# Weights of three pairs by VectorE shifts, and the last three pairs weighed in two halves, in a decayed-neighbour graph layer

## The chip, the cores and the metric

The kernel runs on one core of one Trainium2 chip. The metric is the device time of one execution in microseconds (us). The core's engines run side by side, each through its own instructions in order: TensorE (PE) multiplies matrices and transposes, VectorE (DVE) and ScalarE (ACT) work element by element, GpSimd (POOL) does small work in on-chip memory (SBUF), and SyncE (SP) issues DMA transfers. Matmul results land in PSUM, an accumulation memory of a few banks of 512 fp32 columns.

## The reference

```python
def layernorm(x, eps=1e-5):                    # no scale, no shift
    return (x - mean) / sqrt(var + eps)

h = maximum(layernorm(x), 0)                   # x: 4096 x 64
support = h @ weight                           # weight: 64 x 64
mask = (adj != 0)                              # adj: 4096 x 4096, fp32
rank = cumsum(mask, axis=1)
deg = rank[:, -1:]
k = minimum(deg, 100)
pos = rank - (deg - k)
w = mask * where(pos > 0, 0.5 ** (k - pos), 0)
out = x + (w @ support + bias)
```

Each row of `adj` marks neighbours. The last neighbour of a row (highest column) has weight 1, the one before it 1/2, then 1/4, and so on, up to 100 neighbours. The weight of an entry is thus two to the minus (number of neighbours to its right). `adj` is 67 MB in fp32 and is read once; everything else is small.

## The kernel before, in words

**Tiling.** The 4096 rows form 8 groups (g = 0 to 7) of 512 rows, each of four row tiles of 128. The columns are cut in two halves of 2048, and the right half of a group is taken before the left. A group's half is a unit: 16 units u = 0 to 15. A unit is fetched by four loads of 1 MB, one per row tile, so there are 64 loads (n = 0 to 63; loads 60 to 63 belong to unit 15). All loads go out on SP's queue, into a ring of eight buffers (`a_sb`). A load waits until the conversion of the load eight places earlier has freed its buffer.

**Stages of one load.** `convert` (line 339 on VectorE, or line 337 on ScalarE for the numbers listed in `signed`) turns 128x2048 floats into mask bytes. `transpose` (line 350, TensorE) turns four bytes at a time, `settle` (lines 359 and 361, VectorE) copies the result from PSUM to the unit's mask tile `mt`.

**Stages of one unit.** `totals` (line 367, TensorE) counts neighbours in sub-blocks. `split` (line 377, ScalarE) and `divide` (line 380, VectorE) each copy one byte plane of the counts out of PSUM; both read the same bank. For a left half, `carry` (line 386, GpSimd) brings in the count of the right half. `suffix` (line 394, TensorE) sums the counts to the right, `clamp` (line 398, VectorE) limits them. `place` (lines 405 and 410, TensorE) then makes, for four "pairs" of column blocks at once, the number of neighbours to the right of every entry: a PSUM tile `v` per pair, in which two bytes of each word are wanted. A unit has eight pairs, k = 0 to 7, so two places. `weigh` (line 415, ScalarE) turns one pair, 128 x 1024 bytes, into weights `wk` with one Exp instruction. `aggregate` (line 427, TensorE) multiplies a pair's weights by `hr`, the support matrix held as two float32r parts, in two matmuls that add to the group's PSUM bank `acc`. There are five `v` buffers, twelve `wk` buffers, two PSUM buffers under tag "t" (transposes, totals, suffix and output share them), and one `acc`.

**End of a group.** `drain` (lines 438 and 440) copies `acc` to SBUF and adds the bias, `turn_back` (line 447, TensorE) transposes it, `finish` (lines 454 and 455, VectorE) adds the two parts to x. `store` sends the rows out. The last group is drained in two halves, half 0 by ScalarE and half 1 by VectorE, and its two output transfers go out on ScalarE's and SP's queues (line 457).

**Setup.** Meanwhile x is turned (`turn`, `turned`), centred, squared, its variance spread and rooted, multiplied by the weight (`support`), scaled, and split into the parts of `hr` (`first`, `second`). `warm` runs matmuls on a tile of zeros where the plan leaves TensorE idle.

**Order.** A planner in the kernel's own Python decides the order of all instructions before anything runs. Each step is a `task` with an engine, a rank (its place in the stream plus the tables `shift` and `own`), a planned duration and the tasks it needs. The planner repeatedly takes the engine that can start earliest, and on it the task of lowest rank that is ready within a tolerance (`wait`). What comes out is one fixed instruction order per engine. At run time an engine waits at its next instruction until what that needs is there, and everything behind it waits too.

## Time and profile before

| | |
|---|---|
| median of 4 runs | 193.21 us (193.17 to 193.81) |
| profiled execution | 193.29 us |
| its span in the trace | 191.6 us, so 1.7 us lie outside it |
| TensorE busy | 171.5 us (90%) |
| ScalarE busy | 167.5 us (87%), of it 133.0 us in 128 weighs |
| VectorE busy | 153.6 us (80%), of it 81.5 us in 59 conversions |
| GpSimd busy | 12.9 us (7%) |
| moved by DMA | 69.47 MB, mean 363 GB/s over the span |

A group of instructions is named by line, engine and tile; "mean" is the duration of one. In a run of equal instructions the next one starts a little before the one ahead of it has ended, so the spacing of a run is somewhat below the mean duration. The "idle before" of an instruction names what released it. Times such as 168.58 are microseconds from the start of the span.

### The profile page before, as it was taken

How to read it: one execution, taken by the hardware profiler on the slowest of the kernel's cores; microseconds unless marked ns; L12 is line 12 of the kernel's file. 1: busy time of each engine (PE TensorE's matmuls, PEld its weight loads, DVE VectorE, ACT ScalarE, POOL GpSimd, SP SyncE). 2: the span in 40 equal slices, each digit the busy share in tenths (PEclk: the TensorE clock that was granted, in tenths of full speed). 3: DMA queues.
4: the chain of work that ended last, by engine and by line, in shares of the span. 5: the costliest groups of instructions: out<-in, count | busy, mean ns of one | idle time of the engine just before them, and what ended most of it. 6: DMA issues, size and time to landing. Idle time of an engine off the chain costs nothing.

```text
span 191.6 us, 3737 instructions
## 1 busy us (share of the span) xinstructions
PE 171.5 (90%) x1473; PEld 101.3 (53%) x1475; DVE 153.6 (80%) x213; ACT 167.5 (87%) x178; POOL 12.9 (7%) x54
## 2 busy tenths in 40 slices
PE   7799995979999998799999997999999789998971
PEld 2475982435546564556455545465555444664630
DVE  4851479999999988998899979999997999954012
ACT  2379988889899999999969999898699899889970
POOL 7000240100010002000000010000100000001000
PEclk9999999999999999999999999999999999999995
DMA  6999999999999999999999999999999999700200
GB/s 217 416 421 426 414 424 416 424 414 419 424 412 426 421 414 424 421 417 423 419 417 417 428 416 423 423 412 424 417 417 421 416 426 416 318 14 0 82 0 27
DMA packets 10337, 69.47 MB, mean 363 GB/s; under 512 B 1360, under 2 KB 1616, under 8 KB 2128
## 3 DMA queue, kind: packets, MB, share of 16 engines
q1 hardware_dynamic: 10016, 69.15, 87.3%
q8 instruction: 11, 0.18, 0.4%
q10 hardware_dynamic: 304, 0.10, 0.2%
q14 instruction: 6, 0.05, 0.1%
HBM read 68.19 MB, written 1.05 MB: 361 GB/s over the span
## 4 chain that ended last, share of the span: by engine, by line
PE 42%; DVE 27%; ACT 12%; DMA 9%; issue 5%; POOL 3%; ACTq 0%; POOLq 0%; DVEq 0%
PE acc L427 15%; DVE m L339 12%; DMA a_sb<-in_adj_dram 9%; ACT wk L415 9%; PE pt L350 9%; DVE mt L361 5%; PE v L410 4%; PE v L405 4%; ACT sums L377 2%; DVE sums L380 2%; PE pc L263 2%; PE tot L367 2%; PE pd L279 2%; PE po L447 1%; DVE behind L398 1%
## 5 line engine op out<-in xcount | busy, mean ns | idle before, releaser
L415 ACT ACTIVATE wk<-v,floor 128x1024 fp32r<-128x1024 uint8 x128 | 133.0, 1125 | 6.7 <-PE v L410 6.5
L339 DVE TENSOR_SCALAR m<-a_sb 128x2048 uint8<-128x2048 f32 x59 | 81.5, 1385 | 6.0 <-DMA a_sb<-in_adj_dram 6.0
L427 PE MATMUL acc<-wk,hr 128*128 128x512 f32 x256 | 77.9, 423 | 1.6 <-ACT wk L415 0.5
L427 PEld LDWEIGHTS acc<-wk,hr 128*128 128x128 f32 x256 | 43.8, 189 | 15.2 <-issue 5.0
L350 PE MATMUL pt<-ident,m 128*128 128x128 f32 x256 | 41.5, 282 | 6.7 <-DVE m L339 3.1
L361 DVE COPY mt<-pt 128x512 uint32<-128x512 uint32 x59 | 40.1, 680 | 5.7 <-PE pt L350 5.7
L350 PEld LDWEIGHTS pt<-ident,m 128*128 128x128 f32 x256 | 27.8, 141 | 27.2 <-issue 9.6
L405 PE MATMUL v<-behind,where 32*128 32x512 f16 x128 | 15.6, 383 | 1.5 <-DVE behind L398 1.4
L386 POOL COPY sums<-behind 1x512 f16<-1x512 f16 x8 | 5.6, 705 | 141.6 <-ACT sums L377 141.6
L380 DVE CAST sums<-tot 128x512 f16<-128x512 uint8 x16 | 10.9, 684 | 5.0 <-ACT sums L377 4.2
L410 PE MATMUL v<-mt,tri 32*32 32x512 f16 x512 | 14.3, 394 | 0.0
L337 ACT ACTIVATE m<-a_sb 128x2048 int8<-128x2048 f32 x5 | 12.6, 2528 | 0.5 <-DMA a_sb<-in_adj_dram 0.5
L398 DVE TENSOR_SCALAR behind<-ps,excess 128x512 f16<-128x512 f32 x16 | 11.8, 741 | 1.2 <-PE ps L394 1.2
L377 ACT ACTIVATE sums<-tot 128x512 f16<-128x512 uint8 x16 | 9.6, 598 | 2.9 <-DVE sums L380 2.1
L394 PE MATMUL ps<-sums,later 128*128 128x512 f16 x32 | 9.7, 381 | 1.5 <-POOL sums L386 1.4
L367 PE MATMUL tot<-mt,band 128*32 128x512 f16 x128 | 10.2, 393 | 0.4
L410 PEld LDWEIGHTS <-tri 32*32 32x32 f16 x512 | 4.4, 87 | 10.3 <-issue 10.3
L246 PE MATMUL none<-junk 128*128 128x512 bf16 x24 | 8.4, 497 | 1.3 <-DVE junk L131 1.2
L405 PEld LDWEIGHTS <-where 32*128 32x128 f16 x128 | 3.6, 91 | 9.5 <-issue 9.4
L258 ACT ACTIVATE xt<-px 64x512 f32<-64x512 f32 x8 | 4.2, 586 | 4.6 <-PE px L254 4.5
L438 DVE TENSOR_SCALAR acc_part<-acc,bias_sb 128x256 f32<-128x256 f32 x1 | 0.5, 483 | 9.5 <-PE acc L427 9.5
L447 PE MATMUL po<-ident,acc_sb 128*128 128x128 f32 x30 | 4.9, 285 | 2.6 <-ACT acc_sb L440 2.4
(82 smaller groups left out, 81.9 us busy)
## 6 DMA issues: line engine op xcount, KB each, us to landing
a_sb<-in_adj_dram SPq DMA_DIRECT2D x64, 1024.0 KB, 16.7
xr<-in_x_dram SPq DMA_DIRECT2D x2, 512.0 KB, 6.3
out_dram<-xr SPq DMA_DIRECT2D x1, 512.0 KB, 18.7
out_dram<-xr SPq DMA_DIRECT2D x1, 384.0 KB, 2.3
out_dram<-xr ACTq DMA_DIRECT2D x1, 64.0 KB, 1.6
out_dram<-xr SPq DMA_DIRECT2D x1, 64.0 KB, 1.6
w<-in_L_gnn_weight_dram ACTq DMA_DIRECT2D x2, 16.0 KB, 5.9
bias_sb<-in_L_gnn_bias_dram SPq DMA_DIRECT2D x1, 0.2 KB, 17.5
```

The lines of the kernel that those rows point to most:

```text
L337: nc.scalar.activation(m_v.bitcast(I8), a_v, AF.Sign)
L339: nc.vector.tensor_scalar(m_v, a_v, 0.0, 64.0, op0=ALU.not_equal, op1=ALU.add)
L350: nc.tensor.transpose(pts[n][:, c, :], m32[:, c * P:(c + 1) * P], ident)
L361: nc.vector.tensor_copy(mw, pt)
L367: nc.tensor.matmul(tot[SUB * c:SUB * (c + 1), :], band[:, SUB - 12 - 4 * a:2 * SUB - 12 - 4 * a], masks[u][:, c, :, a], start=(a == 0), st ...
L377: nc.scalar.activation(*bytes_of(u, 0), AF.Copy)
L380: nc.vector.tensor_copy(*bytes_of(u, 1))
L398: nc.vector.tensor_scalar(behind[u], pts.pop((u, "s")), excess[UNITS[u][2]], float(MAX_NEIGH), op0=ALU.subtract, op1=ALU.min)
L405: nc.tensor.matmul(v, where[q, a, :], behind[u][q, :], start=True, stop=False, skip_group_check=True)
L410: nc.tensor.matmul(vs[u, 4 * a + j][SUB * c:SUB * (c + 1), :], tri[q, q], m, start=False, stop=True, skip_group_check=True)
L415: nc.scalar.activation(wts[u, k], vs.pop((u, k)).bitcast(U8).rearrange("p (i f) -> p f i", f=4)[:, :2, :], AF.Exp, scale=-LN2, bias=floor)
L427: nc.tensor.matmul(accs[g], hr[:, block(u, k) + 4 * s, :, :].rearrange("p s d -> p (s d)"), wk[:, s, :], start=(k == s == 0 and c0 + cb * ...
```

## The change

ScalarE no longer weighs three of the last sixteen pairs: pair 4 of unit 14 and pairs 0 and 4 of unit 15 (`QUICK`). For each of them VectorE makes the weights in three instructions. `encode` multiplies the counts by -2^23 and limits them at -100 x 2^23, as 32-bit integers; `cut` adds 100 x 2^23; the bits of that integer, read as a float, are a power of two. `take` copies it into a float32r weight tile. The weights come out too large by a fixed power of two, so `lower`, on GpSimd, makes copies of the `hr` blocks of these pairs that are smaller by it, in a freed load buffer, and `gather` aggregates with those.

Pairs 5, 6 and 7 of unit 15 (`PARTED`) are weighed and aggregated in two halves of the 512 rows: first half 0 of all three, then half 1.

Further edits go with it: ScalarE converts two loads in place of five; the turned x lies in a mask buffer and not in a load buffer; the variance lies in the `acc` bank; `support` waits for `power`; the warming matmuls have 256 columns and end at the first `spread`; the planner has new tables and tolerances, so that the order of many instructions moves. The tables `shift` and `own` are replaced as a whole and are left out of the diff.

```diff
+    QUICK = (U - 2, 4), (U - 1, 0), (U - 1, 4)
+    PARTED = 5, 6, 7
...
-    xt = apool.tile([P, N // H], F32, tag="a_sb", name="xt")
+    xt = mpool.tile([P, CB, W, 2], F16, name="mt").rearrange("p c i e -> p (c i e)").bitcast(F32)
...
-    junk = setup.tile([P, W], BF16, name="junk")
+    junk = setup.tile([P, 2 * P], BF16, name="junk")
...
-            nc.tensor.matmul(none, junk[:, :P], junk, start=True, stop=True)
+            nc.tensor.matmul(none[:, :2 * P], junk[:, :P], junk, start=True, stop=True)
...
-            pxs["var"] = ps_v.tile([P, W], F32, tag="v", name="pd")
+            pxs["var"] = ps_a.tile([P, W], F32, tag="acc", name="pd")
...
-    masks, words, wts, accs, tots, pts, sums8, behind, vs, signed = {}, {}, {}, {}, {}, {}, {}, {}, {}, (2, 3, 5, 6, 12)
+    low, codes, masks, words, wts, accs, tots, pts, sums8, behind, vs, signed = {}, {}, {}, {}, {}, {}, {}, {}, {}, {}, {}, (2, 8)
...
-    def weigh(u, k):
+    def weigh(u, k, part=None):
+        r = slice(0, W) if part is None else slice(part * W // 2, (part + 1) * W // 2)
+        if not part:
+            wts[u, k] = wpool.tile([P, 2, W], F32R, name="wk")
+        v = vs[u, k] if part == 0 else vs.pop((u, k))
+        nc.scalar.activation(wts[u, k][:, :, r], v.bitcast(U8).rearrange("p (i f) -> p f i", f=4)[:, :2, r], AF.Exp, scale=-LN2, bias=floor)
+
+    def encode(u, k):
+        both = apool.tile([P, N // H], F32, tag="a_sb", name="code")
+        codes[u, k] = both.rearrange("p (n f i) -> p n f i", n=2, f=2)
+        nc.vector.tensor_scalar(codes[u, k][:, 0].bitcast(I32), vs.pop((u, k)).bitcast(U8).rearrange("p (i f) -> p f i", f=4)[:, :2, :],
+                                -2.0 ** 23, -100 * 2.0 ** 23, op0=ALU.mult, op1=ALU.max)
+
+    def cut(u, k):
+        nc.vector.tensor_scalar(codes[u, k][:, 1].bitcast(I32), codes[u, k][:, 0].bitcast(I32), 100 * 2.0 ** 23, None, op0=ALU.add)
+
+    def take(u, k):
         wts[u, k] = wpool.tile([P, 2, W], F32R, name="wk")
-        nc.scalar.activation(wts[u, k], vs.pop((u, k)).bitcast(U8).rearrange("p (i f) -> p f i", f=4)[:, :2, :], AF.Exp, scale=-LN2, bias=floor)
+        nc.vector.tensor_copy(wts[u, k], codes.pop((u, k))[:, 1])
+
+    def lower(u, k):
+        if not low:
+            both = apool.tile([P, N // H], F32R, tag="a_sb", name="low").rearrange("p (n s e d) -> p n s e d", s=2, e=2, d=D)
+            low.update((uk, both[:, i]) for i, uk in enumerate(QUICK))
+        for s in range(2):
+            nc.gpsimd.tensor_scalar(low[u, k][:, s, :, :], hr[:, block(u, k) + 4 * s, :, :].bitcast(F32), 2.0 ** -11, None, op0=ALU.mult)
...
-    def aggregate(u, k):
+    def aggregate(u, k, part=None):
...
+        wk = wts[u, k] if part == 0 else wts.pop((u, k))
+        r = slice(0, W) if part is None else slice(part * W // 2, (part + 1) * W // 2)
         for s in range(2):
+            parts = low[u, k][:, s, :, :] if (u, k) in QUICK else hr[:, block(u, k) + 4 * s, :, :]
+            nc.tensor.matmul(accs[g][:, r], parts.rearrange("p s d -> p (s d)"), wk[:, s, r],
...
+    def gather(u, k):
+        aggregate(u, k)
...
     shift = ...
     own = ...
...
-        slot = ("center", 3) if n == NA - 1 else ("convert", n - NA) if n >= NA else None
+        slot = ("convert", n - NA) if n >= NA else None
...
-        task(support, (n,), PE, -3.5, 890, 1090, [("relu", n)], ("v", ("scale", n)))
+        task(support, (n,), PE, -3.5, 890, 1090, [("relu", n), ("power",)], ("v", ("scale", n)))
...
+            if u == U - 1 and k in PARTED:
+                continue
...
+            if (u, k) in QUICK:
+                weighs = "take"
+                task(encode, (u, k), DVE, due - 8, 1150, 1270, [("place", u, k // 4), ("convert", NT - 2)])
+                task(cut, (u, k), DVE, due - 8, 650, 770, [("encode", u, k)])
+                task(take, (u, k), DVE, due - 8, 650, 770, [("cut", u, k)], ("w", ("gather", u, k)))
+                task(lower, (u, k), POOL, due - 8, 1200, 1300, [("second", piece_of // 2, piece_of % 2), ("convert", NT - 3)])
+            else:
+                task(weigh, (u, k), ACT, due + 2.5, 1000, 1130, [("place", u, k // 4)], ("w", ("aggregate", u, k)))
...
+        for part in range(2 if u == U - 1 else 0):
+            for k in PARTED:
+                due = at + k + part
+                task(weigh, (u, k, part), ACT, due + 2.5, 520, 650, [("place", u, k // 4)], None if part else ("w", ("aggregate", u, k, 1)))
+                task(aggregate, (u, k, part), PE, due + 14, 260, 500, [("weigh", u, k, part)])
...
-                    task(drain, (g, part), DVE if part else ACT, at, 300, 350, [("aggregate", u, 2 * cb - 1)])
+                    task(drain, (g, part), DVE if part else ACT, at, 300, 350, [("aggregate", u, PARTED[-1], part), *(("gather", *uk) for uk in QUICK)])
...
-    wait = 400, 250, 250, 60, 0
+    wait = 250, 60, 250, 60, 0
...
-                warm(int(at - end) // 430)
-            end = None if f is aggregate or end is None else at + tasks[f.__name__, *args][4]
+                warm(int(at - end) // 215)
+            end = None if f is spread or end is None else at + tasks[f.__name__, *args][4]
```

## The prediction

> **What bounds the kernel now.** I read the page's slices first, then the busy time by stages, then SP's waits, then the instructions in order of time from 160 us on. In the slices (40 of 4.8 us):
>
> ```profile
> DVE  4851479999999988998899979999997999954012
> ACT  2379988889899999999969999898699899889970
> DMA  6999999999999999999999999999999999700200
> ```
>
> DMA is full from the second slice to the 34th, then nearly silent for the last five. Stages (after the window and its length: busy time of each engine with its instruction count, the granted clock, DMA share, GB/s):
>
> ```profile
> 20.00:40.00 20.00, 17.17 (x160) 12.21 (x160) 16.38 (x25) 18.27 (x21) 4.33 (x14) 1.00 1.01 419
> 140.00:160.00 20.00, 18.04 (x167) 10.15 (x165) 18.51 (x23) 19.21 (x21) 0.60 (x1) 1.00 1.01 419
> 171.60:185.20 13.60, 12.11 (x89) 7.07 (x88) 2.29 (x4) 13.46 (x14) 0.60 (x1) 1.00 0.07 29
> ```
>
> The share is 1.0 and 419 GB/s in both windows of the stream: 64 loads of 1.049 MB at that rate are 160 us, and no order of the engines shortens them. In the last window ScalarE has no gap (13.46 of 13.60) and VectorE almost nothing (2.29). SP's waits say how far the loads are from the engines:
>
> ```profile
> SPq L118 <- DVE m L339: 89.3, 48, 2.9
> ```
>
> SP waits 48 times for a conversion to free a buffer, yet the stream never starves: the last load is issued at 149.8 and lands 18.4 later, so over seven loads stand ahead of it. It lands at about 168.4; the tail of 23 us is what can change. Its instructions (start, duration, ..., count, idle before and releaser):
>
> ```profile
> 168.58 1.40 DVE L339 TENSOR_SCALAR m<-a_sb 128x2048 uint8<-128x2048 f32 x1
> ...
> 170.79 0.69 DVE L361 COPY mt<-pt 128x512 uint32<-128x512 uint32 x1 [0.81 <-PE pt L350]
> ...
> 171.53 0.64 PE L367 MATMUL tot<-mt,band 128*32 128x512 f16 x8
> 171.60 1.11 ACT L415 ACTIVATE wk<-v,floor 128x1024 fp32r<-128x1024 uint8 x1 [0.57 <-PE v L410]
> ...
> 172.61 0.59 ACT L377 ACTIVATE sums<-tot 128x512 f16<-128x512 uint8 x1
> ...
> 173.24 0.69 DVE L380 CAST sums<-tot 128x512 f16<-128x512 uint8 x1 [1.75 <-ACT sums L377]
> 173.26 0.60 POOL L386 COPY sums<-behind 1x512 f16<-1x512 f16 x1 [19.83 <-ACT sums L377]
> ...
> 174.55 0.75 DVE L398 TENSOR_SCALAR behind<-ps,excess 128x512 f16<-128x512 f32 x1 [0.62 <-PE ps L394]
> 174.66 10.45 ACT L415 ACTIVATE wk<-v,floor 128x1024 fp32r<-128x1024 uint8 x10
> ...
> 185.16 0.74 PE L427 MATMUL acc<-wk,hr 128*128 128x512 f32 x2 [0.27 <-ACT wk L415]
> 185.93 0.48 DVE L438 TENSOR_SCALAR acc_part<-acc,bias_sb 128x256 f32<-128x256 f32 x1 [9.52 <-PE acc L427]
> 186.51 0.47 ACT L440 ACTIVATE acc_sb<-acc,bias_sb 128x256 f32<-128x256 f32 x1 [1.40 <-DVE acc_part L438]
> 187.04 0.44 PE L447 MATMUL po<-ident,acc_sb 128*128 128x128 f32 x2 [1.14 <-ACT acc_sb L440]
> ...
> 188.90 0.33 SPq L457 DMA_DIRECT2D out_dram<-xr  x1
> ```
>
> The last load is converted as it lands (168.58). From 171.60 ScalarE works through twelve weighs, a split and a drain without a pause until 185.11, while clamp(15) is done at 175.30: ScalarE sets the end, VectorE idles 9.52.
>
> **The Trainium skill.** "VectorE: DVE Perf Modes", the perf-mode tier table: single-source fp32 copies and tensor_scalar in SBUF pass two elements a cycle at 0.96 GHz, with a PSUM operand fp32 passes one. The trace agrees: a conversion of 2048 from SBUF takes 1.385 us (1.07 + 0.32), a cast of 512 from PSUM 0.68 (0.53 + 0.15). "PSUM — Partial Sum Buffer", section on bank collisions: two engines must not touch one bank at once, so programs order them. The trace shows it: L440 idles 1.40 behind L438, L380 1.75 behind L377, though both only read.
>
> **The change, part by part.** Spacings: a weigh 1.04 ((10.45 - 1.12)/9); an aggregate pair 0.5 to issue (a run of ten matmuls takes 2.56), 0.73 alone; a transposition 0.11 to issue (four in 0.63, one in 0.28); a place 0.78 from start to result (175.90 to 176.67).
>
> *New VectorE work.* encode reads 1024 bytes per partition from PSUM: 1.07 + 0.15 = 1.22. cut and take stay in SBUF: 0.53 + 0.15 = 0.68 each, between 0.6 and, at one element a cycle, 1.22. With 0.03 between dependent ones, 2.64 a pair, 7.9 in all, inside the 9.5 of idleness. lower, six GpSimd instructions of 128 elements, is under 0.7 each (L386 moves 512 in 0.70), 4.2 in all; as built it starts after conversion 56 (near 152) and is wanted at 177: free, and without that cover 4.2.
>
> *ScalarE.* Three weighs less: -3.1. Six half weighs for three whole: 0.52 each, at most 0.6 (L377's 512 elements), so 0 to +0.5.
>
> *The landing chain.* As built, VectorE settles load 62 after conversion 63 (hidden under its transposes until 170.75). TensorE turns group 6 back and issues the first pair of group 7 ahead of totals(15): from 170.78, 4 x 0.11 + 2 x 0.25, so totals starts 171.75 instead of 171.53, ends 172.39. Group 6's finish (0.9) fits before it. Then divide goes before split: divide 172.42 to 173.10, split (ScalarE reads the same bank, so as built it waits for divide) 173.15 to 173.75, carry 173.80 to 174.40, suffix (0.59) to 175.05, clamp 175.10 to 175.85: +0.55. Queued behind split, ScalarE waits from about 172.6 (split(14), four weighs of unit 13, two of 14, a drain, two more). It resumes at 173.65 with (14,5), (14,6), (14,7), the last ending 176.85. Place(15,0) stands behind the pairs of (14,3), (14,5) and (14,6): (14,6) ends 175.81, its pair issues to 176.36, place is ready at 177.2. ScalarE waits another 0.4.
>
> *Last weighs.* (15,1) 177.2, (15,2) 178.24 to 179.36, (15,3) 179.28, halves from 180.32 spaced 0.52: the last ends 183.52 (before: 185.11). Place(15,1) needs (15,2)'s buffer: 179.41 + 0.78 = 180.2, just in time. encode(15,4) 180.2 to 181.42, cut to 182.13, take to 182.84. TensorE takes that pair in fifth place from the end, 182.9 to 183.4, a half pair (LDWEIGHTS 0.19 each, so 0.38 at most to issue) to about 183.75, then the last half pair, some 0.3 until its result: `acc` complete about 184.05 against 185.90, **-1.85**.
>
> *The end.* In the program as built half 0's drain waits for the last matmul of half 1 too, and VectorE's drain waits for it (one bank); so the halves do not let it start early. ScalarE drain 184.08 to 184.55, VectorE drain 184.65 to 185.13, finish of half 0 (0.29 twice) to 185.77; half 1's turn_back, as built, waits for that: 185.83 to 186.22; its finish to 186.88; SP issues at 186.92 against 188.90: **-1.98**. The output transfer behind it (2.7 to the end) is as before.
>
> *The fill.* ScalarE loses three early conversions (3 x 2.53), VectorE gains them (3 x 1.27 spaced). xt, the variance's bank, junk, `support`'s wait and load 7's lost wait lie there too. I cost them at nothing: the stream covers them, with VectorE idle 6 of 10 us at 10 to 20 us and some 3 of 20 to 40. Without that cover up to 3.8.
>
> Sum: profiled 193.29 - 1.98 = 191.3; the median stood 0.08 below, so **191.2 us**.
>
> **Rivals.**
> (B) *cut and take run at one element a cycle.* Each costs 0.53 more; encode(15,4) then waits for take(15,0), starts 181.0 and take ends 184.6; `acc` completes at 185.9, and no more than 0.1 to 0.2 is gained: 193.1. For it: no row shows int32 or float32r output from SBUF. Against: L339 passes two a cycle into another type.
> (C) *Slower: the load stream gets a hole in the fill.* A load's buffer is freed by the conversion eight places earlier. With 18 us of queue, a conversion more than about 16 us behind its landing (or a settle or transposition stuck in the new order ahead of it) stops DMA, and each us of hole is a us at the end. Past 2.0 of hole the gain is eaten, past 2.6 it is slower beyond what can be told; with all 3.8 us of the uncovered conversions it ends at 191.2 + 3.8 = 195.0. Against: VectorE's idleness there, and 20 us of VectorE at 140 to 160 hold 18.5 busy, so it catches up. For: new order everywhere, and VectorE is 9 in nearly every slice.
> (D) *The landing chain runs faster than I count*, or the stream ends earlier because load 7 goes out at once: up to 1 us, 190.2. Against: the stream's share is already 1.0.
> (E) *The change does not do what it says*: the halves are already counted so above (no drain starts early). If VectorE's third pair, and not the last weigh, releases the last aggregates, each 0.1 that encode, cut or take is dearer is 0.1 at the end; B is its far end, so it has no chance of its own.
>
> **How the numbers follow.** Forecast 0.70, with a range of its own of 190.5 to 192.0 (half weighs +0.5, chain waits 0.3 each way); B 0.08; C 0.12; D 0.10. Forecast and D reach 0.80: 190.2 to 192.6, where the top holds the dearer halves (+0.5) and half of B's price together. A run of this kernel tells about 0.3% (0.58 us) from no change. Faster: A and D, 0.80. Same: B, 0.08. Slower: C, 0.12.
>
> **What would show it.** Right: the last load landing at 168 to 169; three weighs fewer in the last run; ScalarE idle ahead of L377's successor, behind DVE; 0.4 idle behind L410; VectorE's new rows at 1.2, 0.7, 0.7; the last weigh ending near 183.5 and SP's output issue near 187. Wrong: a DMA slice below 9 before the 34th; cut or take near 1.2; the half-weigh row above 0.65; `acc` waiting for take and not for the weigh.

## The result and the profile after

The changed kernel takes 192.88 us (median of 36 runs, 191.93 to 193.62) against 193.31 us for the kernel before on the same chip (55 runs): a ratio of 0.9951, 95% interval 0.9936 to 0.9967. It is faster: by 0.4 us in the medians, by 0.9 us by the ratio (14 of the 55 runs of before lie between 194.7 and 195.3 us, which its median doesn't show), where the forecast had 2.0. The forecast of 191.2 is too low by 1.7 us, and 192.88 lies above its range. Executions in a slow state of the chip, two of e4 below, are left out of all figures.

The profiled execution took 192.54 us, with a span of 190.8 us. The slices of its page that answer to those of before, with the granted TensorE clock in tenths (PEclk) added:

```profile
DVE  4853886999999998999999988999999999988753
ACT  2289219999897899889987999989989799998880
PEclk9999859999999999999999999999999999999998
DMA  5999999999999999999999999999999999802000
```

DMA is full as before. VectorE now works through the tail (the last slices read 988753 where before they read 954012). ScalarE has a hole in slices 5 and 6. PEclk has a dip in the same place, which the page of before did not have: there the row was 9 up to the last slice. The clock is granted in full or in half, and at half from 22.2 to 29.0 us here.

Busy time by stages (columns: window and its length, then PE, PEld, DVE, ACT and POOL busy with instruction counts, granted clock, DMA share, GB/s), of the kernel after:

```profile
20.00:40.00 20.00, 18.50 (x146) 13.09 (x147) 17.52 (x24) 12.08 (x14) 5.32 (x14) 0.83 1.01 419
140.00:160.00 20.00, 18.48 (x171) 10.56 (x170) 19.69 (x25) 17.43 (x19) 4.93 (x6) 1.00 1.01 418
```

At 20 to 40 us ScalarE has 12.08 us of work where it had 18.27, and the clock is 0.83 where it was 1.00. At 140 to 160 us VectorE is busy 19.69 of 20.

The tail, in order of time (start, duration, engine and line, ..., count, idle before and releaser). L341 is the conversion, L379 split, L382 divide, L420 weighs, L426 encode, L400 clamp, L473 the drain on ScalarE, L480 turn_back:

```profile
162.01 1.40 DVE L341 TENSOR_SCALAR m<-a_sb 128x2048 uint8<-128x2048 f32 x1
...
164.00 0.60 ACT L379 ACTIVATE sums<-tot 128x512 f16<-128x512 uint8 x1 [0.27 <-DVE sums L382]
...
168.28 1.39 DVE L341 TENSOR_SCALAR m<-a_sb 128x2048 uint8<-128x2048 f32 x1
170.57 0.69 ACT L473 ACTIVATE acc_sb<-acc,bias_sb 128x512 f32<-128x512 f32 x1
...
173.12 0.69 DVE L382 CAST sums<-tot 128x512 f16<-128x512 uint8 x1 [0.23 <-PE tot L369]
173.79 1.22 DVE L426 TENSOR_SCALAR code<-v 128x1024 int32<-128x1024 uint8 x1
173.84 0.60 ACT L379 ACTIVATE sums<-tot 128x512 f16<-128x512 uint8 x1 [0.58 <-DVE sums L382]
...
175.78 0.75 DVE L400 TENSOR_SCALAR behind<-ps,excess 128x512 f16<-128x512 f32 x1
...
178.12 6.68 ACT L420 ACTIVATE wk<-v,floor 128x1024 fp32r<-128x1024 uint8 x9 [0.66 <-PE v L412]
...
185.39 0.47 ACT L473 ACTIVATE acc_sb<-acc,bias_sb 128x256 f32<-128x256 f32 x1 [0.59 <-PE acc L457]
...
187.06 0.44 PE L480 MATMUL po<-ident,acc_part 128*128 128x128 f32 x2 [0.71 <-DVE xr L488]
...
188.18 0.33 SPq L490 DMA_DIRECT2D out_dram<-xr  x1
```

The shape of the tail is the one forecast: divide ahead of split, ScalarE waiting 0.58 behind it, three whole and six half weighs at the end, the second half's turn_back behind the first half's finish. SP issues the output at 188.18, against 188.90 before and 186.92 in the forecast.

Three spans worked out from the traces sort all that follows. **Debt** is how long after its load has landed a conversion starts, as a mean over loads 54 to 61; at a single load this is called how far VectorE is behind it. **c63** is the start of the last conversion. **Tail** is from c63 to SP's last output issue. Before: debt 0.17, c63 168.58, tail 20.32. After: debt 1.23, c63 168.28, tail 19.90. The forecast's tail was 186.92 - 168.58 = 18.34: 1.56 us is missing there, and c63 itself came 0.3 earlier.

### The profile page after: what moved, and what is told of

The parts are those of the page before. It is cut to its first block, busy times and chain, and to the rows that moved or that the text cites. A ratio compares the mean times of both kernels' runs of the same rounds, so it can differ in the third digit from the quotient of the medians.

```text
span 190.8 us, 3811 instructions
## 1 busy us (share of the span) xinstructions
PE 172.3 (90%) x1504; PEld 106.5 (56%) x1504; DVE 165.6 (87%) x225; ACT 158.1 (83%) x175; POOL 19.7 (10%) x60
## 4 chain that ended last, share of the span: by engine, by line
PE 45%; ACT 14%; DVE 13%; issue 12%; DMA 8%; POOL 7%; POOLq 0%; ACTq 0%; DVEq 0%
PE acc L457 16%; ACT wk L420 11%; PE pt L352 9%; DMA a_sb<-in_adj_dram 8%; DVE m L341 5%; PE v L412 4%; PE v L407 4%; POOL low L443 3%; PE tot L369 2%; PE pd L281 2%; DVE mt L363 2%; PE ps L396 2%; PE pc L265 2%; PE px L256 2%; DVE xs L307 1%
## 5 line engine op out<-in xcount | busy, mean ns | idle before, releaser
L420 ACT ACTIVATE wk<-v,floor 128x1024 fp32r<-128x1024 uint8 (+1 forms) x128 | 130.2, 1101 | 13.3 <-PE v L412 13.0
L341 DVE TENSOR_SCALAR m<-a_sb 128x2048 uint8<-128x2048 f32 x62 | 86.2, 1391 | 2.5 <-DMA a_sb<-in_adj_dram 2.5
L457 PE MATMUL acc<-wk,hr 128*128 128x512 f32 (+1 forms) x256 | 78.5, 421 | 1.5 <-ACT acc_sb L473 0.9
L352 PE MATMUL pt<-ident,m 128*128 128x128 f32 x256 | 42.4, 286 | 6.8 <-DVE m L341 2.8
L363 DVE COPY mt<-pt 128x512 uint32<-128x512 uint32 x62 | 42.2, 681 | 5.9 <-PE pt L352 5.8
L352 PEld LDWEIGHTS pt<-ident,m 128*128 128x128 f32 x256 | 28.6, 144 | 25.0 <-issue 7.9
L379 ACT ACTIVATE sums<-tot 128x512 f16<-128x512 uint8 x16 | 9.6, 599 | 5.2 <-DVE sums L382 2.7
L400 DVE TENSOR_SCALAR behind<-ps,excess 128x512 f16<-128x512 f32 x16 | 11.9, 743 | 0.8 <-PE ps L396 0.7
L382 DVE CAST sums<-tot 128x512 f16<-128x512 uint8 x16 | 10.9, 684 | 1.6 <-ACT sums L379 0.9
L248 PE MATMUL none<-junk 128*128 128x256 bf16 x49 | 7.8, 330 | 1.1 <-DVE junk L133 1.1
L260 ACT ACTIVATE mt<-px 64x512 f32<-64x512 f32 x8 | 4.2, 586 | 4.9 <-PE px L256 4.8
L248 PEld LDWEIGHTS <-junk 128*128 128x128 bf16 x49 | 5.7, 118 | 3.1 <-DVE junk L133 1.1
L473 ACT ACTIVATE acc_sb<-acc,bias_sb 128x512 f32<-128x512 f32 (+1 forms) x8 | 5.3, 664 | 1.5 <-PE acc L457 1.4
L480 PE MATMUL po<-ident,acc_sb 128*128 128x128 f32 x30 | 4.8, 280 | 1.4 <-ACT acc_sb L473 1.4
```

The lines of the kernel that those rows point to most:

```text
L248: nc.tensor.matmul(none[:, :2 * P], junk[:, :P], junk, start=True, stop=True)
L341: nc.vector.tensor_scalar(m_v, a_v, 0.0, 64.0, op0=ALU.not_equal, op1=ALU.add)
L352: nc.tensor.transpose(pts[n][:, c, :], m32[:, c * P:(c + 1) * P], ident)
L363: nc.vector.tensor_copy(mw, pt)
L382: nc.vector.tensor_copy(*bytes_of(u, 1))
L400: nc.vector.tensor_scalar(behind[u], pts.pop((u, "s")), excess[UNITS[u][2]], float(MAX_NEIGH), op0=ALU.subtract, op1=ALU.min)
```

## The experiments

Each kernel was timed beside the kernel before. The clock in the table is the mean granted TensorE clock of the profiled execution. It differs between executions of one program, and within the kernel after the time follows it, so medians are also compared at like clock below. What the means stand for shows in the traces of the kernels made from the kernel after. Profiles with a mean of 0.973 or less have two stretches of half clock, 6.8 us near 24 us and 3.4 us near 44 us; those from 0.977 to 0.982 have only the first; those from 0.996 on have neither. The bands below 0.977, from 0.977 to 0.983 and from 0.99 on thus compare executions of one pattern, as far as the profiles show it. They don't hold across kernels: beside f0 the kernel before took 194.86 us in its 18 runs from 0.977 to 0.983, where f0 took 192.60.

Runs e0 to e8 were made on one chip, e9 to e12 on a second, f0 to f3 on a third, g1 and g2 on the first. The kernel after ran beside e1 to e3 and f1 to f3 only; the others are compared with it across batches or chips.

| kernel | median us (runs) | ratio to before, 95% interval | clock | debt | c63 | tail |
|---|---|---|---|---|---|---|
| e0_after, control | 192.79 (22) | 0.996 [0.994, 0.9979] | 0.972 | 1.76 | 168.77 | 19.92 |
| e1_no_lower | 192.44 (13) | 0.9931 [0.9904, 0.9957] | 0.972 | 1.34 | 168.24 | 19.93 |
| e2_long_warm | 193.31 (14) | 1.0002 [0.998, 1.0024] | 0.996 | 1.91 | 168.95 | 19.93 |
| e3_whole | 193.10 (22) | 0.9975 [0.9953, 0.9998] | 0.971 | 1.71 | 168.73 | 20.17 |
| e4_two_to_act | 196.97 (4) | 1.0154 [1.0089, 1.022] | 0.977 | 4.69 | 172.03 | 19.92 |
| e5_pe_relief | 192.76 (22) | 0.9951 [0.9927, 0.9976] | 0.965 | 2.63 | 169.31 | 19.93 |
| e6_quick_act | 195.47 (11) | 1.0098 [1.0067, 1.0128] | 0.980 | 1.22 | 167.98 | 22.86 |
| e8_no_scale | 192.30 (11) | 0.9912 [0.9879, 0.9946] | 0.964 | 1.49 | 168.43 | 19.90 |
| e9_no_finish | 192.19 (12) | 0.9899 [0.9866, 0.9933] | 0.967 | 1.21 | 168.35 | 19.91 |
| e12_fill_act | 191.85 (6) | 0.9898 [0.9847, 0.9948] | 0.996 | 0.19 | 167.93 | 19.12 |
| e10_own_bank | 191.92 (6) | 0.9895 [0.9845, 0.9945] | 0.997 | 0.25 | 168.02 | 18.45 |
| e11_all | 191.53 (6) | 0.9879 [0.9826, 0.9933] | 0.981 | 0.69 | 168.00 | 18.82 |
| f0_after, control | 192.93 (22) | 0.9958 [0.9937, 0.9979] | 0.972 | 1.54 | 168.67 | 19.94 |
| f1_debt | 195.44 (9) | 1.0093 [1.0057, 1.0128] | 0.985 | 2.66 | 170.37 | 20.32 |
| f2_fill_act | 192.69 (22) | 0.9938 [0.9914, 0.9961] | 0.973 | 1.77 | 168.79 | 19.95 |
| f3_split_first | 192.05 (19) | 0.9921 [0.9896, 0.9947] | 0.981 | 0.51 | 168.06 | 19.51 |
| g1_best | 190.60 (6) | 0.9856 [0.982, 0.9891] | 0.982 | 0.41 | 168.17 | 18.17 |
| g2_warm | 190.48 (6) | 0.9853 [0.9815, 0.9891] | 1.000 | 0.18 | 168.12 | 17.96 |

The first four runs hold three causes apart: the copies on GpSimd (e1), the half-clock stretch (e2) and the half weighs (e3). From e4 on, "theory 4" is that VectorE got late in the fill and is too full to catch up; the debt above is its measure.

The tail is the first thing to see: 19.9 in every kernel with the change's tail and a debt above 1. The pattern is rigid, and what moves it is the start of conversion 60. From there to SP's last output issue it is 26.17 to 26.21 us in every kernel that leaves the change's tail as it is, with a debt of 0.19 (e12) as with one of 4.69 (e4). A late conversion 60 thus makes the end late by the same amount. With little debt conversion 63 waits for its own load, so c63 can't come earlier with conversion 60, and the tail counted from it gets shorter instead.

### Four suspects of the missing time

**e0_after: the control.**

> The changed kernel itself, on the chip and beside the runs of the three edits below. Theory 1 (the clock sets a part of the time): runs whose mean granted clock is 0.99 take about 192.0 us, runs at 0.97 about 192.9. Rival: the two go without each other.

Measured 192.79, ratio 0.996: the result again.

**e1_no_lower: the scaled copies on GpSimd left out.**

```diff
     def lower(u, k):
-        if not low: ...
-            nc.gpsimd.tensor_scalar(low[u, k][...], hr[...], 2.0 ** -11, None, op0=ALU.mult)
+        return
-            parts = low[u, k][...] if (u, k) in QUICK else hr[...]
+            parts = hr[...]
```

> The six GpSimd instructions of lower are left out, and the three pairs of VectorE are aggregated with the unscaled support, so those terms of the sum are too large; all else and the order are as in the changed kernel. Theory 2 (lower, 5.2 us on GpSimd at 156 to 161 us, holds VectorE up, and so conversion 60, divide(14), split(14) and the drain of group 6 are late): 0.4 to 0.7 us below the changed kernel. Rival (the delay was there before lower began): within 0.2 us of it.

Measured 192.44, 0.35 below its control, and 0.41 below it among the executions with a clock below 0.977 (192.59 against 193.00). The place is visible. In the kernel after, in order of time:

```profile
156.22 2.13 POOL L443 TENSOR_SCALAR low<-hr 128x128 fp32r<-128x128 f32 x2
156.26 1.74 DVE L341 TENSOR_SCALAR m<-a_sb 128x2048 uint8<-128x2048 f32 x1
```

and the same conversion without the copies:

```profile
156.63 1.39 DVE L341 TENSOR_SCALAR m<-a_sb 128x2048 uint8<-128x2048 f32 x1
```

The conversion starts 0.04 us after the first copy and takes 1.74 us, not 1.39. The second copy starts at 156.72, while the conversion runs, and takes 1.63 us where the first takes 0.52. The Trainium skill, "SBUF — State Buffer", section "Who interferes with whom", says that VectorE in a two-port mode and GpSimd contend for one pair of ports, and that the later one blocks for the whole of the other's instruction. The trace agrees: the conversion is longer by 0.35 behind the first copy, and the second copy, which alone would end at 157.24, ends at 158.35, just after the conversion (158.00). At like clock (0.972 in both profiles) c63 is 168.24 against 168.77. The copies are not free.

**e2_long_warm: the warming goes on until the first aggregate, with four more warming matmuls after each spread.**

```diff
+    still = [none]
-            nc.tensor.matmul(none[:, :2 * P], junk[:, :P], junk, ...)
+            nc.tensor.matmul(still[0][:, 2 * P:], junk[:, :P], junk, ...)
-            pxs["var"] = ps_a.tile(...)
+            pxs["var"] = still[0] = ps_a.tile(...)
...
+        warm(4)                                     # at the end of spread
-            end = None if f is spread or ...
+            end = None if f is aggregate or ...
```

> The changed kernel with warming matmuls (256 columns) going on to the first aggregate, and four more behind each spread, all into unused columns of the variance's bank. Theory 1 (the half clock at 22 to 29 us puts the unit pipeline behind, and this is still there in the tail): no half-clock stretch in most runs, mean clock 0.99, median 0.7 to 1.0 us below the changed kernel, near 192.0. Rival (the stream covers the fill, and the low clock is only a sign): clock up, time within 0.2 us of the changed kernel.

The clock came up (all 14 runs at 0.989 or more, where the control has one of 22 there), but the time did not come down: 193.31, so the expectation missed. clamp(0) starts at 26.26 us in place of 25.05, and the debt is 1.91. At load 12 VectorE is 1.0 us further behind its loads than in the control, at load 20 0.3: the additional matmuls cost the fill about what the clock saves it. This run by itself left open what the clock is worth.

**e3_whole: pairs 5, 6 and 7 of unit 15 weighed whole.**

```diff
     def weigh(u, k, part=None):
-        r = slice(0, W) if part is None else slice(part * W // 2, (part + 1) * W // 2)
+        if part == 1: return
+        part, r = None, slice(0, W)
```
(`aggregate` likewise.)

> Pairs 5, 6 and 7 of unit 15 are weighed and aggregated whole again, at the place of their first halves; all else as in the changed kernel. Theory 3 (a half weigh costs 0.59, not 0.52, and no drain starts early): ScalarE ends 0.4 us earlier, the last aggregate takes 0.2 longer, so 0.1 to 0.3 us below the changed kernel. Rival (the halves do shorten the end): 0.3 to 0.6 us above it.

Measured 193.10, 0.31 above the control, and the tail 20.17 against 19.92. ScalarE's end and the drain, of this kernel:

```profile
178.59 6.23 ACT L423 ACTIVATE wk<-v,floor 128x1024 fp32r<-128x1024 uint8 x6 [0.67 <-PE v L412]
...
186.11 0.47 ACT L478 ACTIVATE acc_sb<-acc,bias_sb 128x256 f32<-128x256 f32 x1 [1.28 <-PE acc L462]
```

ScalarE is done 0.45 us sooner with whole pairs (6.23 for six, against 6.68 for three and six halves), but then waits 1.28 us for `acc` instead of 0.59. What follows the last weigh on TensorE is shorter with halves. So they pay, by 0.25 us of tail, and my doubt of them was wrong, although the six of them cost more on ScalarE than three whole ones.

### Is it the middle of the kernel that holds the debt?

**e4_two_to_act: conversions 20 and 36 on ScalarE** (`if n in signed or n in (20, 36)`).

> Conversions 20 and 36 are made by ScalarE, at their planned place in time; all else and the order are as in the changed kernel. Theory 4 (VectorE has next to no slack, so the three conversions that it took over leave it 1 to 1.6 us behind the landings at loads 56 to 61, and so divide(14), split(14) and group 6's drain come late): its lag falls by 2 us or to nothing, conversion 60 starts at about 160.6, and the time is 0.5 to 1.0 us below the changed kernel. Rival (TensorE holds the lag): no lag is recovered, time within 0.2 us or longer by ScalarE's 2 x 2.5 us.

Measured 196.97 (four runs), 3 us slower than before by the ratio; the expectation was far off: the debt is 4.69 and c63 172.03. ScalarE has no room in the middle. VectorE is 0.8 us further behind its loads than in the control after the first of the two conversions (load 22), 2.3 after the second (load 38), and 2.9 at loads 54 to 61: each 2.5 us conversion put there delays all engines for good.

**e5_pe_relief: 48 aggregate matmuls of units 4 to 11 left out.**

```diff
-        for s in range(2):
+        for s in range(1 if 4 <= u < 12 and 0 < k < 7 else 2):
```

> In units 4 to 11 the aggregates of pairs 1 to 6 leave out the second of their two matmuls, so that half of those terms are missing from the sum; TensorE has 48 matmuls, some 12 us, less to do between 65 and 150 us. Theory 4 (VectorE itself is full): the lag behind the landings stays within 0.7 us of the changed kernel's and the end with it. Rival (VectorE is late because it waits for TensorE): the lag falls to nothing by unit 12 and the time by 0.5 to 1.0 us.

Measured 192.76, as the controls of other batches (192.79, 192.93); the debt, 2.63, is not smaller. TensorE's load in the middle does not hold it.

**e9_no_finish: the finishing of groups 1 to 5 left out**, that is the two additions of each, 4.3 us less for VectorE.

```diff
     def finish(g, part=None):
+        if 1 <= g <= 5: return
```

> The kernel after, with the finishing (two additions of 0.43 us on VectorE, and the subtraction ahead of them) of groups 1 to 5 left out: their rows of the output aren't the reference's, and VectorE has about 5 x 0.87 = 4.3 us less to do between 77 and 155 us. Theory 4 (the three conversions moved to VectorE in the fill put it 2 to 3 us behind the loads, and it is too full to catch up): conversions at loads 54 to 61 begin at least 1 us nearer their landings than in the kernel after (1.0 to 1.6 behind there), conversion 60 starts by 161.2, and the time is 0.5 to 0.9 us below the kernel after (192.8): 191.9 to 192.3. Rival (VectorE only follows a rhythm that ScalarE and the order set): conversion 60 stays within 0.3 us of the kernel after, and the time within 0.2 us of it.

Conversion 60 starts at 162.07, against 162.41 and 162.49 in the two controls: the 1 us of the theory did not come. The time is 0.5 lower at a clock below 0.977 (192.5, against 193.0 to 193.1 for the controls, on other chips). Some 4 us taken from VectorE repay at most 0.5 of the debt. That VectorE is too full is thus at most a part of it; that the order shared with the other engines is the rest was not shown by a run of its own.

### What the change's own parts are worth

**e6_quick_act: the three pairs weighed by ScalarE again, in the new order, without the copies** (`encode` calls `weigh`; `cut`, `take` and `lower` return).

> The three pairs are weighed by ScalarE again, at the place in time of encode; cut, take and lower are left out, and the sum is as in the reference. The order is otherwise the changed kernel's. If VectorE's weights are what gains: three weighs of 1.04 come back to ScalarE, less the 1.2 us in which it waits in the tail and less 0.4 for the missing lower, so 1.3 to 2.0 us above the changed kernel, that is 0.6 to 1.1 above the kernel before. Rival (the new order of the rest gains): within 0.5 us of the changed kernel.

Measured 195.47, 0.7 more than expected at the highest, and the tail 22.86. VectorE's weights are worth 2.9 us in this order (22.86 - 19.90 = 2.96 of tail), close to the 3.1 forecast for three weighs less. But the same order without them is slower than before (ratio 1.0098, 1.9 us), its tail 2.54 longer (22.86 - 20.32). Most of what the three weighs give is spent on what the new order of the tail costs.

**e8_no_scale: 89 for 100 in `encode` and `cut`, so that the weights come out with no factor, and no copies.**

```diff
-                                -2.0 ** 23, -100 * 2.0 ** 23, op0=ALU.mult, op1=ALU.max)
+                                -2.0 ** 23, -89 * 2.0 ** 23, op0=ALU.mult, op1=ALU.max)
-        nc.vector.tensor_scalar(codes..., 100 * 2.0 ** 23, None, op0=ALU.add)
+        nc.vector.tensor_scalar(codes..., 89 * 2.0 ** 23, None, op0=ALU.add)
     def lower(u, k):
+        return
```

> lower is left out, and 89 in place of 100 in encode and cut gives weights of the right size at once (those below 2 to the -88 become zero), so that the sum is as in the reference. Theory 2 (lower holds VectorE up by 0.4 us): as with lower left out, 0.3 to 0.5 us below the changed kernel, near 192.4. Rival: within 0.2 us of it.

Measured 192.30, ratio 0.9912 [0.9879, 0.9946], 0.5 below the control of the first batch. It confirms e1 with a kernel that needs no scaled copies. From here on this edit is kept in the combined kernels.

**e10_own_bank: e8, and half 1's turn_back in a PSUM tile of its own.**

```diff
-        if ("o", g) not in pts:
-            pts["o", g] = ps_t.tile([P, TG, 2, D], F32, tag="t", name="po")
+        if ("o", g, part) not in pts:
+            pts["o", g, part] = ps_t.tile([P, TG, 2, D], F32, tag="t", name="po")
```

> The kernel after without the scaled copies on GpSimd (89 instead of 100 in the encoding, the same weights exactly) and with the last turn-back of the second half in a PSUM tile of its own, so that it doesn't wait for the finishing of the first half. The wait of the last drain's copy to the first transpose of the second half is then 0.1 to 0.2 us instead of 0.7: the output's DMA is issued 0.5 us earlier. Expected 191.8 (191.5 to 192.1), against 192.3 without the second edit. Rival (VectorE's two halves follow each other, so that the second waits for the first on its own engine): the time stays at 192.3.

Measured 191.92. The end of it, in order of time:

```profile
184.30 0.47 ACT L469 ACTIVATE acc_sb<-acc,bias_sb 128x256 f32<-128x256 f32 x1 [0.60 <-PE acc L453]
...
185.35 0.44 PE L476 MATMUL po<-ident,acc_part 128*128 128x128 f32 x2
...
186.47 0.33 SPq L486 DMA_DIRECT2D out_dram<-xr  x1
```

From drain to issue it takes 2.17 us where the kernel after takes 2.79 (185.39 to 188.18): turn_back no longer waits 0.71 behind L488. At a clock of 0.99 or more it runs 190.92 (one run) against 191.50 for e8 (three, on another chip).

### Where the debt comes from

**e12_fill_act: conversions 5 and 6 back on ScalarE.** TensorE's order stays the same.

```diff
-        if n in signed:
+        if n in signed or n in (5, 6):
```
(in `convert` and in `settle`, not in the planner.)

> The kernel after, with conversions 5 and 6 back on ScalarE, which stands idle for 6.1 us in the fill before 28.1 us; everything else as after. Theory 4: VectorE is 2.5 us less behind its loads at loads 6 and 7 (3.0 and 4.6 us after), the gain is kept through the rigid rhythm of the middle, conversion 60 starts within 0.6 us of its landing, and the time is 0.5 to 0.9 us below the kernel after: 191.9 to 192.3. Rival (the fill's debt is repaid or irrelevant by load 54, or ScalarE is made late instead): within 0.2 us of the kernel after, or above it.

**e11_all: e10 with this edit too.**

> As the run with the tile of its own, and conversions 5 and 6 on ScalarE too. If theory 4 holds, another 0.5 to 0.9 us below it: 190.9 to 191.3. If the fill's debt doesn't matter: the same 191.8.

e12 ran at 191.85, and its profile has no debt (0.19) and a tail of 19.12. e11 ran at 191.53, less gain over e10 than expected; at like clock it is 0.6 to 0.7 below e10 (191.91 against 192.54 below 0.977; 191.18 against 191.92 at 0.977 to 0.983), on two or three runs each. That looked like the answer. But e12's profile had a clock of 0.996, so the kernel was run once more beside a control.

**f0_after and f2_fill_act: control, and the kernel of e12 again, on one chip.**

> The kernel after, unchanged, as control on the chip of the other three: 192.5 to 192.9 us, conversion 60 at 162.0 to 162.5, and VectorE 1.0 to 2.2 us behind the landings of loads 54 to 61.

> The kernel after with conversions 5 and 6 on ScalarE, beside its control on the same chip. Debt: 0.6 to 0.8 us below the control. Clock alone (the earlier run's gain came from its full clock): within 0.2 us of the control at the same granted clock.

192.69 against 192.93: only 0.24. At like clock f2 is 0.15 lower below 0.977 (192.94 against 193.09), 0.5 at 0.977 to 0.983 (192.08 against 192.60), 0.4 at 0.99 and more (191.66 against 192.02). The two conversions are worth some 0.3 us, less than half of what I put on them. The larger part shows between two profiles of this one program. First f2's, with a mean clock of 0.973:

```profile
PEclk9999957996999999999999999999999999999999
...
26.98 2.08 PE L304 MATMUL pp<-w,rx 128*128 128x128 f32 x8
28.85 1.06 PE L352 MATMUL pt<-ident,m 128*128 128x128 f32 x4
...
30.55 1.40 DVE L341 TENSOR_SCALAR m<-a_sb 128x2048 uint8<-128x2048 f32 x1
```

Then e12's, with 0.996, from another chip:

```profile
PEclk9999999999999999999999999999999999999998
...
26.10 1.16 PE L304 MATMUL pp<-w,rx 128*128 128x128 f32 x8
27.09 0.60 PE L352 MATMUL pt<-ident,m 128*128 128x128 f32 x4
...
29.46 1.37 DVE L341 TENSOR_SCALAR m<-a_sb 128x2048 uint8<-128x2048 f32 x1
```

At half clock the same eight matmuls of `support` (L304) take 2.08 us for 1.16, and four transpositions 1.06 for 0.60. VectorE waits for both, and conversion 7 starts 1.1 us later. The slow row has a second dip, the 6 in the tenth slice: the clock is at half from 23.9 to 30.8 us, and again from 44.4 to 47.8. VectorE is further behind its loads than in the other profile by 1.9 us at load 17, 2.4 at load 18, and 2.4 to 2.7 from there to load 50. Nothing gives the delay back in time: conversion 60 starts at 162.53 against 160.88, c63 is 168.79 against 167.93, the tail 19.95 against 19.12, and the time 193.12 against 191.42 us. The same program is 1.7 us apart, and the two stretches of half clock are where the two traces part.

e8 and e10 are a second such pair, with conversions 5 and 6 where the change put them: one program up to the last turn_back, on two chips. Their rows, e8 (0.964) first, then e10 (0.997):

```profile
PEclk9999957996999999999999999999999999999996
PEclk9999999999999999999999999999999999999998
```

The debt is 1.49 and 0.25, and conversion 60 starts at 162.16 and 160.90. VectorE in e8 is 0.3 us further behind at load 17, and 1.0 from load 18 to load 50, so most of it comes at the second stretch. With no half clock the debt is nearly gone here too, though the conversions are still on VectorE.

The kernel after shows the first stretch in its profile (22.2 to 29.0 us), and 23 of its 36 runs have a clock below 0.98, 18 of them below 0.977. In its six runs at 0.99 and more it takes 191.95, and the three such runs of f0 192.02, where the kernel before took 192.92 in eleven beside them. At full clock the change is thus worth 0.9 us. The Trainium skill, "TensorE: Matmul & The Clock Gate", Part 1, says that half clock is the state of a TensorE that has not been busy for a window of 3.4 us, that the window runs freely, and that the penalty varies from run to run. The lengths here, 6.8 and 3.4 us, are two windows and one, and the coming and going between runs of one program agrees too. The idle window doesn't show: in the 3.4 us ahead of the first stretch TensorE is busy by the profile for 3.40 in e8, and as much in e10, which keeps its clock; ahead of the second it is busy for 1.56 in e8 and 1.55 in e10. Why the changed kernel meets half clock more often was not isolated: both a shorter warming and a thinner fill are in the change. Nor does any run change the clock and nothing else; that it costs the time rests on the two pairs, on the longer matmuls that VectorE waits for, and on the runs sorted by clock.

**f1_debt: the kernel before with conversions 5 and 6 on VectorE, and nothing else.**

```diff
-        if n in signed:
+        if n in signed and n not in (5, 6):
```

> The kernel before, with conversions 5 and 6 on VectorE in place of ScalarE, and nothing else of the change; TensorE's order is the same. If a debt made in the fill is kept to the end: VectorE 1 to 2.5 us more behind its loads from load 8 on, some of it still there at loads 54 to 61 (0 to 0.5 in the kernel before), and 0.3 to 0.9 us slower than before (193.2): 193.5 to 194.1. If VectorE, which has 12 us less to do in this kernel, pays it back: within 0.2 us of before.

Measured 195.44, ratio 1.0093: 1.8 us slower than before, more than either theory had. The debt rises from 0.17 to 2.66, c63 from 168.58 to 170.37, and the tail stays at 20.32 to the hundredth. The last conversion and the issue of the output in f1 (before: 168.58 and 188.90):

```profile
170.37 1.40 DVE L339 TENSOR_SCALAR m<-a_sb 128x2048 uint8<-128x2048 f32 x1
...
190.69 0.33 SPq L457 DMA_DIRECT2D out_dram<-xr  x1
```

VectorE, busy 80% in that kernel, does not catch up in 140 us. It is 2.8 us further behind its loads than before at load 7, 2.7 to 3.0 from there to load 50, and 2.5 at load 60. Its profile has 3.4 us of half clock from 33.9 us on, but conversion 7 starts at 32.70, so the delay is older. A delay made in the fill is kept to the end: this is the plainest of the runs.

It shows that a delay is kept, not how large the change's is. In the kernel after the same two conversions are worth the 0.3 us of f2. In f2's profile VectorE is 2.3 us less behind than in the control at load 6, but only 0.4 at load 7, where it waits for the matmuls at half clock, and no less from load 9 on.

### The landing chain

**f3_split_first: f2, and split(15) ahead of divide(15), divide waiting for it.**

```diff
     def divide(u):
+        split(u, u == U - 1) if u == U - 1 else None      # and split does nothing at its own turn for unit 15
         nc.vector.tensor_copy(*bytes_of(u, 1))
```

> As the run with conversions 5 and 6 on ScalarE, and for unit 15 ScalarE's split reads the bank of totals before VectorE's divide does, and divide waits for it; the instructions and their order on every engine are the same. ScalarE's wait of 0.58 us for divide is gone, carry starts 0.6 us earlier, clamp(15) 0.4 to 0.5 us earlier. Expected 0.3 to 0.5 us below that run. Rival (the chain to place is bound by TensorE's order, not by the two reads): within 0.15 us of it.

192.05 against 192.69, but at like clock only 0.03 to 0.2 (192.05 against 192.08 at 0.977 to 0.983), and 0.13 from conversion 60 to SP's issue (26.07 against 26.20 in f0). The landing chain of this kernel, in order of time:

```profile
172.64 0.62 ACT L379 ACTIVATE sums<-tot 128x512 f16<-128x512 uint8 x1
173.29 0.69 DVE L382 CAST sums<-tot 128x512 f16<-128x512 uint8 x1 [0.90 <-ACT sums L379]
...
173.90 1.22 DVE L426 TENSOR_SCALAR code<-v 128x1024 int32<-128x1024 uint8 x1
175.15 0.69 DVE L431 TENSOR_SCALAR code<-code 128x1024 int32<-128x1024 int32 x1
175.76 0.74 DVE L400 TENSOR_SCALAR behind<-ps,excess 128x512 f16<-128x512 f32 x1
```

ScalarE's wait is gone, but clamp (L400) is no earlier: it stands on VectorE behind encode and cut (L426, L431) of pair (14,4), and these follow divide without a gap. Counted from conversion 60 clamp starts after 14.25 us, and after 13.77 to 13.80 in the kernels with divide first, since divide itself is now later. One wait was removed and the next took its place.

**g1_best: e11, split first, and that cut behind clamp(15).**

```diff
     def clamp(u):
         ...
+        cut(U - 2, 4, True) if u == U - 1 else None       # and cut does nothing at its own turn for (14, 4)
```

> The combined kernel (no scaled copies on GpSimd, own PSUM tile for the last turn-back, conversions 5 and 6 on ScalarE) with split(15) ahead of divide(15), and with VectorE's cut of pair (14,4) behind clamp(15) in place of ahead of it. If that cut is what took over the wait: clamp(15) starts 0.6 to 0.7 us nearer to the start of conversion 63 than in the run with split first (7.70 us there), ScalarE's wait for place falls from 1.0 to 0.3 or 0.4 us, and the time is 190.4 to 190.7 us at a clock near 0.98 (191.2 without these two edits). If place is held by TensorE's order: within 0.2 us of 191.2.

```profile
168.17 1.40 DVE L341 TENSOR_SCALAR m<-a_sb 128x2048 uint8<-128x2048 f32 x1 [0.52 <-DMA a_sb<-in_adj_dram]
...
174.76 0.74 DVE L400 TENSOR_SCALAR behind<-ps,excess 128x512 f16<-128x512 f32 x1
175.42 0.68 DVE L430 TENSOR_SCALAR code<-code 128x1024 int32<-128x1024 int32 x1
...
176.90 6.68 ACT L420 ACTIVATE wk<-v,floor 128x1024 fp32r<-128x1024 uint8 x9 [0.66 <-PE v L412]
...
186.34 0.33 SPq L485 DMA_DIRECT2D out_dram<-xr  x1
```

clamp(15) starts 6.59 us after conversion 63 (7.69 in f3). Part of that is f3's debt; counted from conversion 60 it is 13.52 us, against 14.25 in f3 and 13.78 in the kernel after. The time is 190.60 us, ratio 0.9856 [0.982, 0.9891]: 2.7 us below the kernel before beside it. ScalarE's wait for place stayed at 0.66, where I expected 0.3 to 0.4. The last conversion again waits for its load (0.52 <-DMA), yet the end still goes with conversion 60: SP issues 25.11 us after it, and 25.12 in g2, where conversion 60 starts 0.27 earlier.

**g2_warm: g1 with seventeen more warming matmuls, seven between 24.0 and 26.7 us and ten from 34.3** (the warming's end as in e2, without the four after each spread).

> As g1_best, but the warming goes on until the first aggregate where the plan leaves TensorE idle: seven more matmuls of 256 columns on zeros between about 22 and 30 us. If the half-clock stretch in the fill makes the larger part of the debt: the granted clock is 0.99 or more in most runs, VectorE is 1 us less behind at load 7, and the median is 0.5 to 0.9 us below g1_best. If the warming stands in the way as in the longer warming before: the same as g1_best or slower.

190.48: no different from g1 within what six runs tell. Two of its six runs have a clock of 0.99 or more, as in g1, so these matmuls don't hold the clock. At full clock both take 190.4. In its profile VectorE is 2.2 us behind at load 7 where g1 has 3.7, and by loads 54 to 61 both have little debt left. What is paid off before the last load lands costs nothing.

## Why the prediction was wrong

**The stream.** "No order of the engines shortens them", last landing about 168.4: right. The share stayed at 1.0, the landing came at 167.9. Rival C, a hole in the stream, did not occur; of rival D, the earlier end of the stream came, by 0.3 us, but the landing chain ran slower and not faster.

**encode, cut and take.** 1.22, 0.68 and 0.68 forecast; 1.22, 0.69 and 0.69 measured. Rival B fell. That int32 and float32r results from SBUF come at the rate of two elements a cycle that the prediction took for them is now measured.

**The end.** From the last weigh's end (184.80) to SP's issue 3.38 us, forecast 3.40. Right within 0.02, with drains and halves in series as predicted.

**"The fill. I cost them at nothing: the stream covers them."** This is the step that failed. The stream does cover it, as far as DMA goes, but DMA was the wrong thing to look at. I wrote that VectorE "catches up" in the middle, from 18.5 of 20 us busy. In f1 two conversions moved to VectorE in the fill cost 1.8 us in the kernel before, with the DMA share at 1.01 in the windows of 20 to 40 and 140 to 160 us. In the kernel after the debt has several sources. The largest is TensorE's half clock in the first 50 us, for which the prediction has no term: 1.7 us between two profiles of one program, and 0.9 of the 1.7 us by which the forecast was too low, as the kernel's median is 192.88 and its runs at full clock take 191.95. The conversions (some 0.3) and the copies below are the smaller ones. What brings the half clock on stays open.

The debt reaches the end by conversion 60 and split(14). Both of them in the kernel before, then both and the output's issue in e12, which has no debt:

```profile
161.34 1.39 DVE L339 TENSOR_SCALAR m<-a_sb 128x2048 uint8<-128x2048 f32 x1
...
163.33 0.60 ACT L377 ACTIVATE sums<-tot 128x512 f16<-128x512 uint8 x1 [0.50 <-DVE sums L380]
```

```profile
160.88 1.39 DVE L341 TENSOR_SCALAR m<-a_sb 128x2048 uint8<-128x2048 f32 x1
...
162.87 0.60 ACT L379 ACTIVATE sums<-tot 128x512 f16<-128x512 uint8 x1 [0.27 <-DVE sums L382]
...
187.05 0.33 SPq L490 DMA_DIRECT2D out_dram<-xr  x1
```

In the kernel after all three come 1.13 us later than in e12, at 162.01, 164.00 and 188.18: the weighs of unit 13, the drain of group 6 and totals(15) stand behind split(14). Of the 1.13 us, 0.35 are in c63, which e12's own load holds at 167.93, and 0.78 in the tail (19.90 - 19.12).

**"lower ... free."** It started at 156.2, not near 152, and cost 0.35 to 0.5 us (e1, e8): it makes one conversion 0.35 longer, on an engine without slack there. I looked for GpSimd's own deadline and not for what its operands share.

**The landing chain.** The order was right, the sizes 0.44 short: with no debt and c63 at 167.93, e12 has split at 172.71 (0.2 later than forecast, counted from c63) and ScalarE resuming at 176.99, another 0.23 later. I charged the divide-before-split order with 0.55 us; f3 shows that reversing it alone gains 0.2 at most, since VectorE's encode and cut of (14,4) stand ahead of clamp(15). In the working I had VectorE's new work "inside the 9.5 of idleness" and did not place it against clamp. With the cut behind clamp and the split first (g1), the output is issued 25.11 us after conversion 60, against 25.52 in e11 without the two. The waits of 1.40 and 1.75 that I read as one reader of a bank behind the other are whole idle times: the second reader starts 0.58 after L438 does and 0.63 after L377, and the rest is from before the first one started.

**Half weighs.** 0.52 forecast, at most 0.6. The last nine weighs take 6.68 where the forecast had 6.32: +0.36. The six halves are 3.58 us of that, 0.60 each, the upper end of the range. e3 shows that the halves pay all the same, 0.25 us of tail, through the shorter work behind them.

**The sum.** The landing chain and the half weighs alone, 0.8 us, would have left 192.0, inside the range; with the fill the median is outside. In the profiled execution SP's issue came 1.26 later than forecast: -0.30 (c63: the stream ended earlier, which only rival D had, and the debt there took back 0.35), +0.78 (debt in the tail), +0.44 (landing chain), +0.36 (half weighs), -0.02 (end). The median lies 0.34 above that execution; 18 of the 36 runs have a lower clock, below 0.977 against its 0.979. The gain of the three weighs themselves, 2.9 us in e6, was near the 3.1 forecast.

## What to carry to other kernels

A fixed order on every engine is a chain of clocks: a delay that one engine gets early is handed round and kept until an engine has to wait for something else, here a load, so "the engine idles later" does not repay it. Ask which engine starts how late after each transfer, not only whether the transfers are covered, and follow one load from the fill to the tail. When work moves to an engine with idle time, place each new instruction against the one that is wanted next on that engine, and against what shares its memory port.

## What I had not expected of the hardware

- A mean granted clock 2% lower cost almost 1% of the time here, although TensorE is not what sets the end: 193.12 and 191.42 us at 0.973 and 0.996 for one program. The half clock lay in the first 50 us, and what VectorE lost there to late matmuls was still missing at the end.
- A GpSimd instruction of 128 x 128 floats takes 0.52 us alone and 1.63 when it starts during a conversion on VectorE; a conversion that starts during such a copy goes from 1.39 to 1.74.
- A conversion with nothing to wait for but its landing starts 0.1 us after it; in the kernel after, at loads 54 to 61, it starts 1.2 us after, and of a delay that was 4.6 us at load 7, 130 us earlier, that is all that shows.
